# Turned maxima behind the products with v, an end in written order, and products beside the first steps of a fused block

## The chip, the cores and the metric

The kernel runs on one core of a Trainium2 chip. The metric is the device time of one execution in microseconds (us); lower is better. An execution is told by five engines that run side by side: PE (matrix products; PEld is its weight load), DVE (vector), ACT (scalar, activations), POOL (general), and SP, which only starts transfers here. Data lie in SBUF; PE writes only into the eight banks of PSUM, 128 x 512 numbers of 32 bits each, and DVE or ACT read them from there. All numbers are 32-bit floats.

## The reference

The input x has 8 batches of 1024 tokens of 256 features. One block with modulated layer norm is computed:

```python
mod = (silu(c) @ wmod).reshape(8, 6, 1, -1)
sa, ca, ga, sb, cb, gb = (mod[:, i] for i in range(6))
ga, gb = (sign(g) * max(abs(g), 0.25) for g in (ga, gb))
h = layernorm(x) * (1 + ca) + sa
x = x + ga * attention(h)        # 16 heads of 16, causal softmax, w_out, b_out
h = layernorm(x) * (1 + cb) + sb
x = x + gb * ffn(h)
# ffn: xp = x shifted by one token
# r = sigmoid((mu_r*x + (1-mu_r)*xp) @ Wr.T)
# k = relu((mu_k*x + (1-mu_k)*xp) @ Wk.T)**2 ; out = r * (k @ Wv.T)
```

## The kernel before

**Attention in units and steps.** A unit is four heads of one batch, so there are 32 units, 28 to 31 in the last batch (number 7). A unit's 1024 tokens are two chunks of 512 (c = 0 and 1). The scores are computed twice. `maxima` (pp) forms them with queries on the partitions and DVE takes each query's largest (`max`). `subtract` turns these maxima: a PE transpose into a bank (pmx), a copy with the sign turned to a row on ACT (mrow), and a small transfer that writes the row into row 16 of each head's strip of q, where k holds ones. `weights` (pw) then forms the scores with keys on the partitions, already less the maximum, and ACT takes the exponential from the bank into a tile w. `attend` multiplies w by v, extended by a column of ones that gives the sum (po), and copies the bank to a tile o on ACT, or to `more`, which POOL adds to o.

A unit takes nine steps, named a, b, c, d, e (pieces on the diagonal) and 0 to 3 (whole tiles). The maxima run LAG = 9 steps ahead of the weights, so a step as a rule holds the weights of one unit and the maxima of the next. Step numbers are counted from the first step of a batch's weights, 36 to a batch. The group of products with v that a step completes is written in the step after it (steps with c, e, 1 and 3; po_c, po_e and po). The last two units have other pieces (f, g, h, i) and groups.

**What stands in a step** (function `step`, line 1022): transfers that have come due (a transfer asked for by `later` goes out at the head of a later step, the rows of maxima first); the products of weights and maxima, in halves; after each half, exponentials and reductions; then the list `soon` (turned maxima among it, one step after the maxima are complete); then the fills of that step from the tables; then the products with v of the step before (`finish`, which calls `attend`). Maxima of chunk 0 are complete after the fifth step of the maxima, those of chunk 1 after the ninth. In every unit both turns fall into a step that also holds a group of products with v.

**Fills.** The rest of the block is cut into small pieces that tables place into numbered steps: START, PREP and PREP_FIRST (norm, turning, q, k, v of the next batch), POST, POST_LAST and END (projection py, second norm, mixing, receptance pr, key pk, value pkv). In a table, `n.q1` is a product q for the second chunk; x and y stand for the two chunks of the batch worked on. A step with no maxima and no fill gets five small transposes ("heat").

**Banks.** `bank` hands out four banks in rotation (tag t): pw, pmx, po and the fills use them. pp has four others, two to a tile (tag s). After the last maxima, `late` is set, and the fills take theirs from the tag s (`bank_apart`).

**Order.** Inside the steps `strict` is set, and then each engine's instructions are bound to the order in which they are written (class InOrder, line 113); PE is always bound so. The first instructions are bound by `start`. `tail` (line 860), which does the last chunk's projection, norm, mixing, key, value and output in two halves, was written with neither flag: PE follows the written order there, while the order on the other engines was left to the planner.

The first nine steps (LAG) have maxima only and the last nine have weights only. In such steps (`alone`) both halves are written at once.

Of the kernel before, what the change touches and what calls it, by code (L numbers as in the profile page):

```python
# [8 lines left out]
F32 = mybir.dt.float32  # L9
# [63 lines left out]
def adaln_block(  # L73
# [293 lines left out]
    def normalise(xt, S, tag, half):  # L367
        if half == 0:
            S["h"] = sb.tile([P, NT, D], F32, tag="h", bufs=2, name=f"h{tag}")
        h, mv, rs = S["h"], S["mv"], S["rs"]  # L370
        for t in (2 * half, 2 * half + 1):
            if strict[0]:
                act.activation(
                    h[:, t, :],
                    xt[:, t, :],
                    AF.Identity,
                    bias=S["away"][:, t : t + 1],
                    scale=rs[:, t : t + 1],
                )
            else:  # L380
                dve.tensor_scalar(
                    h[:, t, :],
                    xt[:, t, :],
                    mv[:, t, 0:1],
                    rs[:, t : t + 1],
                    ALU.subtract,
                    ALU.mult,
                )

    def transposed(h, to, b, d, shift, scale, name):  # L390

        pt = bank(name)
        for t in range(NT):
            pe.transpose(
                pt[:, t * P : (t + 1) * P], h[:, t, d * P : (d + 1) * P], ident
            )
        by, at = modT[:, scale, d, b : b + 1], modT[:, shift, d, b : b + 1]
        if d and shift == SHIFT_A:
            dve.tensor_scalar(to, pt, by, at, ALU.mult, ALU.add)
        else:  # L400
            act.activation(to, pt, AF.Identity, bias=at, scale=by)
# [246 lines left out]

    def attend(u, k):

# [10 lines left out]
        for m, (at, kt, lo, cols) in enumerate(parts):  # L661
            for j in range(HG):
                pe.matmul(
                    po[j * ST : (j + 1) * ST, lo:],
                    v_tile(b, kt)[:, (g * HG + j) * (HD + 1) :][:, :ST],
                    ws[at, j // 2][:, j % 2, cols],
                    start=m == 0,
                    stop=m == len(parts) - 1,
                )
        if ("o", c) not in V:  # L670
            V["o", c] = sb.tile([P, CW], F32, tag="o", bufs=3, name=f"o{u}_{c}")
# [95 lines left out]
    def post(b, c):  # L767
# [57 lines left out]
        def receptance(t0):  # L825
            pr = bank_apart(f"pr{b}_{c}_{t0}")
            rows(pr, S["mix"], wr_sb, (t0, t0 + 1))
            r = sb.tile([P, CW], F32, tag="r", bufs=2, name=f"r{b}_{c}_{t0}")
            act.activation(r, pr, AF.Tanh, scale=0.5)
            S["r", t0] = r  # L830
# [29 lines left out]
        def tail(other):  # L860

            def both(f):
                f(0)
                f(1)

            def columns(half):
                return slice(half * CW // 2, (half + 1) * CW // 2)

            both(lambda half: project(2 * half))
            other["multiplied0"]()
            st = sb.tile([P, NT, 6], F32, tag="st", bufs=2, name="st_last")
            mv = sb.tile([P, NT, 2], F32, tag="mv", bufs=2, name="mv_last")
            rs = sb.tile([P, NT], F32, tag="rs", bufs=2, name="rs_last")
            h = sb.tile([P, NT, D], F32, tag="h", bufs=2, name="h_last")

            def normal(half):
                ts = (2 * half, 2 * half + 1)
                for t in ts:  # L880
# [4 lines left out]
                pool.tensor_tensor(rs[:, of], rs[:, of], m_half[:, of], ALU.pow)  # L885
                if half:
                    pool.tensor_mul(away, mv[:, of, 0], rs[:, of])
                    pool.tensor_scalar_mul(away, away, -1.0)
                for n, t in enumerate(ts):
                    if half:  # L890
                        act.activation(
# [14 lines left out]
                    )  # L906

            away = sb.tile([P, 2], F32, tag="away", bufs=2, name="away_last")
            both(normal)
            h2T = sb.tile([P, DC, CW + 1], F32, tag="h2T", name="h2T_last")  # L910
            pool.tensor_copy(h2T[:, :, 0:1], A[b, 0]["edge"])

# [17 lines left out]

            turned(0)
            other["multiplied2"]()
            turned(1)
            step = sb.tile([P, DC, CW], F32, tag="step", name="step_last")
            S["mix"] = sb.tile([P, DC, CW], F32, tag="mix", bufs=2, name="mix_last")

            def mixed_half(half):
                of = columns(half)
                for d in range(DC):
                    dve.tensor_sub(  # L940
# [3 lines left out]
                    )  # L944
                for n in range(2):
                    for d in range(DC):
                        dve.scalar_tensor_tensor(
                            (S["mix"], step)[n][:, d, of],
                            step[:, d, of],
                            mus[:, n, d : d + 1],  # L950
                            h2T[:, d, of],
                            ALU.mult,
                            ALU.add,
                        )

            both(mixed_half)
            other["valued0"](), other["valued2"]()
            S["ka"] = sb.tile([P, DC, CW], F32, tag="mix", bufs=2, name="ka_last")

# [15 lines left out]

            both(lambda half: (receptance(2 * half), keys(half)))

            def values(half):
                t0 = 2 * half
                pv = bank(f"pkv_last{half}")  # L980
                rows(pv, S["ka"], G[b]["wv"], (t0, t0 + 1))
                r = S["r", t0]
                dve.scalar_tensor_tensor(r, r, 1.0, pv, ALU.add, ALU.mult)
                dve.tensor_add(flat(t0), flat(t0), r)
                (sync, act)[half].dma_start(
                    tokens(out, b, c)[:, t0 : t0 + 2, :], S["x"][:, t0 : t0 + 2, :]
                )

            both(values)

# [28 lines left out]

    soon = []  # L1020

    def step(T, T1, S, now, fill):
# [23 lines left out]
        for f in fill:  # L1046
            f()
        if not S and not fill:

            pt = bank_apart(f"heat{now}")  # L1050
            for n in range(5):
                pe.transpose(pt[:, :P], ident, ident)
        if T1 and T1[1] in groups_of(T1[0]):
            finish(T1, now)
        if S:
            u = S[0]
            for c, _, _ in STEPS[S[1]]:
                left[u, c] = left.get((u, c), PIECES[c]) - 1
                if left[u, c] == 0:
                    join(u, c)  # L1060
                    soon.append((now + 1, lambda c=c: subtract(u, c)))
        soon.sort(key=lambda z: z[0])

    def finish(T, now):
        u, k = T
        attend(u, k)
        c, _, ends = groups_of(u)[k]
# [44 lines left out]
    19 x.receptance0; 19 y.norm1; 20 y.turn; 20 x.receptance2; 20 x.key0; 21 y.mix; 22 x.key1;  # L1112
    22 y.mixed00; 24 y.mixed01; 24 y.mixed10; 24 x.value0; 25 y.mixed11; 26 x.value2;
    28 y.receptance0; 29 y.receptance2; 29 y.key0; 31 y.key1; 33 y.value0; 35 y.value2
    """

    POST_LAST = """
    -12 x.load; -6 x.bias; 4 x.project0; 6 x.project2; 7 x.stats0; 7 y.load; 8 x.stats1; 8 y.bias;
    9 x.norm0; 9 y.project0; 10 x.norm1; 10 x.turn; 11 x.mix; 11 y.project2; 12 x.mixed00;
    12 y.stats0; 13 x.mixed01; 13 x.mixed10; 13 x.receptance0; 14 x.mixed11; 15 x.receptance2;  # L1120
    15 y.stats1; 16 y.norm0; 17 x.key0; 17 y.norm1; 18 x.key1; 18 y.turn; 19 y.mix; 20 x.value0;
    20 y.mixed00; 21 y.mixed01; 21 y.mixed10; 22 x.value2; 22 y.mixed11; 22 y.receptance0;
    23 y.receptance2; 24 y.key0; 25 y.key1; 26 y.value0; 27 y.value2
    """
# [6 lines left out]
    START = """  # L1131
    0 n.turn; 3 m.q1; 4 m.k1; 6 n.q1; 7 n.k1; 8 m.v0; 10 m.v2; 11 n.v0; 13 n.v2
    """
# [3 lines left out]
    12 n.stats1; 13 n.norm0; 14 n.norm1; 15 n.turn; 16 n.q0; 17 n.k0; 19 m.v0; 20 m.v2; 20 m.q1;  # L1137
    22 m.k1; 22 n.q1; 24 n.k1; 29 n.v0; 31 n.v2
    """
    END = """  # L1140
    16 x.load; 18 x.bias; 26 y.load; 28 x.project0; 28 y.bias; 29 x.project2; 30 x.stats0;
    30 x.stats1; 31 x.norm0; 32 x.norm1; 32 x.turn; 33 x.mix; 34 x.mixed00; 34 x.mixed01;
    34 x.mixed10; 34 x.mixed11; 35 x.receptance0; 36 x.receptance2
    """
# [34 lines left out]
    for b in range(B):  # L1179
# [12 lines left out]
        )  # L1192
    place(END, at, x=ready[b][0], y=ready[b][1])

# [57 lines left out]
    finish(order_t[-1], len(slots))  # L1252
    for n, f in ((1, "key0"), (2, "key1")):
        soon.append((len(slots) + n, ready[B - 1][0][f]))
# [61 lines left out]
```

## Time and profile before

| | us |
|---|---|
| median of 3 executions | 1392.13 |
| lowest and highest | 1391.22 and 1395.94 |
| the profiled execution, whole | 1394.23 |
| its span, first to last instruction | 1392.5 |
| PE busy, share of the span | 1362.3, 98% |
| DVE, ACT, POOL busy | 1061.3, 876.1, 545.0 |
| one steady batch (from 383.46 to 547.16, and so on) | 163.7 |
| mean granted clock of PE | 0.996 |

The page gives busy time by engine, and the span in 40 slices with a digit for tenths of busy time. The timeline lists instructions in order of time: start, length, engine, line, operation, the tile written, `<-`, the tiles read, shapes, count, and in brackets the idle time of the engine ahead of it and what ended it. Nearly all instructions carry line 123, that of the helper InOrder, so tiles tell them apart. An end of a matrix product is modelled, and several run at once in parts of the array; the distance between starts tells more than the length. A stretch line gives its length and then busy time and count of PE, PEld, DVE, ACT and POOL, then the granted clock of PE (1.00 is full), the share of the transfer engines, and GB/s.

### The profile page before, as it was taken

The numbers are of one execution on the slowest core, as the hardware profiler recorded it, in microseconds if no ns is written. First come the engines' busy times: TensorE is split into PE (matmuls) and PEld (weight loads), VectorE is DVE, ScalarE is ACT, GpSimd is POOL, SyncE is SP. The second block draws the span as 40 slices with busy tenths as digits, with TensorE's granted clock in tenths as the row PEclk, the third lists the DMA queues.
The fourth block names the chain that finished last, engine by engine and source line by source line (L and its number), as shares of the span: only waits on it lengthen the run. The fifth ranks groups of instructions, "written<-read, shape, count | busy, mean of one in ns | idle before, by whom it ended". The sixth has DMA issues, their size and how long they took to land.

```text
span 1392.5 us, 29440 instructions
## 1 busy us (share of the span) xinstructions
PE 1362.3 (98%) x11093; PEld 751.1 (54%) x11093; DVE 1061.3 (76%) x2872; ACT 876.1 (63%) x1695; POOL 545.0 (39%) x841
## 2 busy tenths in 40 slices
PE   9999999999999999999999999999999999989997
PEld 5554455555555555555555555555555555555545
DVE  6787787788778777788777887778787877877624
ACT  3476676676666666665666666666666666556461
POOL 1142243345423454434434355234543344345432
PEclk9999999999999999999999999999999999999999
DMA  6513323232222323222242222323232222301101
GB/s 193 182 38 97 118 78 115 63 101 88 92 71 75 108 85 107 67 88 80 78 131 63 98 84 71 97 78 108 70 105 56 65 100 78 101 24 37 61 5 35
DMA packets 81582, 118.12 MB, mean 85 GB/s; under 512 B 10136, under 2 KB 39704, under 8 KB 81440
## 3 DMA queue, kind: packets, MB, share of 16 engines
q1 hardware_dynamic: 81104, 115.92, 25.9%
q8 instruction: 87, 1.43, 0.4%
q14 instruction: 55, 0.45, 0.1%
q10 hardware_dynamic: 336, 0.33, 0.1%
HBM read 70.63 MB, written 44.55 MB: 83 GB/s over the span
## 4 chain that ended last, share of the span: by engine, by line
PE 90%; DVE 4%; ACT 3%; POOL 1%; issue 1%; DMA 0%; ACTq 0%; DVEq 0%; POOLq 0%
PE pw L123 11%; PE po L123 8%; PE pq L123 8%; PE pp L123 7%; PE po_c L123 5%; PE po_e L123 5%; PE pr L123 4%; PE py L123 4%; PE pv L123 4%; PE pkv L123 4%; PE pk L123 4%; PE pw_a L123 3%; PE pw_e L123 3%; PE pw_c L123 2%; PE pw_b L123 2%; ACT w L123 2%
## 5 line engine op out<-in xcount | busy, mean ns | idle before, releaser
L123 DVE TENSOR_REDUCE max<-pp 128x2 f32<-128x1024 f32 x256 | 302.3, 1220 | 64.9 <-PE pp L123 64.4
L123 ACT ACTIVATE w<-pw 128x512 f32<-128x512 f32 x512 | 265.7, 602 | 82.8 <-PE pp L123 59.9
L123 PE MATMUL pw<-q,k 32*128 32x512 f32 x1024 | 267.4, 616 | 0.7 <-ACT w_i L123 0.6
L123 PE MATMUL pp<-k,q 32*128 32x512 f32 x1024 | 256.3, 619 | 0.4 <-DVE max L123 0.4
L123 PEld LDWEIGHTS pw<-q,k 32*128 32x128 f32 x1024 | 108.0, 183 | 101.3 <-issue 59.3
L123 DVE DVE_READ_ACCUMULATOR2_ANT max<- 128x1 f32 x1024 | 144.7, 141 | 0.0
L123 DVE CUSTOM_DVE_ANT_0 pp_c<-pp_c,mask 128x256 f32<-128x256 f32 x240 | 102.3, 436 | 42.6 <-PE pp_c L123 36.5
L123 DVE CUSTOM_DVE_ANT_0 pp_b<-pp_b,mask 128x128 f32<-128x128 f32 x240 | 102.3, 437 | 38.3 <-PE pp_b L123 32.1
L123 DVE CUSTOM_DVE_ANT_0 pp_e<-pp_e,mask 128x512 f32<-128x512 f32 x128 | 88.0, 708 | 54.7 <-PE pp_e L123 52.6
L123 DVE CUSTOM_DVE_ANT_0 pp_d<-pp_d,mask 128x128 f32<-128x128 f32 x240 | 102.4, 437 | 30.2 <-PE pp_d L123 24.1
L123 PE MATMUL po<-w,v 128*32 128x512 f32 x1024 | 123.1, 598 | 1.2
L123 PE MATMUL pq<-hT,wqk_sb 128*128 128x512 f32 x240 | 115.3, 613 | 0.0
L123 DVE CUSTOM_DVE_ANT_0 pp_a<-pp_a,mask 128x512 f32<-128x512 f32 x128 | 87.8, 707 | 11.6 <-PE pp_a L123 9.5
L123 POOL TENSOR_TENSOR xb<-xb,r 128x512 f32<-128x512 f32 x30 | 38.9, 1298 | 141.3 <-DVE r L123 116.2
L123 ACT ACTIVATE w_a<-pw_a 128x512 f32<-128x512 f32 x128 | 66.5, 603 | 41.5 <-PE pp_a L123 38.0
L123 POOL TENSOR_TENSOR o<-o,more 128x512 f32<-128x512 f32 x62 | 78.6, 1267 | 35.7 <-ACT more L123 35.6
L123 POOL TENSOR_TENSOR rsb<-rsb,m_half 128x2 f32<-128x2 f32 x30 | 21.4, 714 | 172.3 <-DVE rsb L123 171.0
L123 PEld LDWEIGHTS pp<-k,q 32*128 32x128 f32 x1024 | 83.8, 184 | 6.5 <-DVE max L123 4.5
L123 ACT ACTIVATE w_d<-pw_d 128x512 f32<-128x512 f32 x120 | 62.4, 601 | 22.8 <-PE pp_e L123 20.6
L123 ACT ACTIVATE w_e<-pw_e 128x512 f32<-128x512 f32 x128 | 66.1, 603 | 15.7 <-PE pp_c L123 13.5
L123 ACT ACTIVATE w_b<-pw_b 128x512 f32<-128x512 f32 x120 | 62.0, 602 | 18.5 <-PE pp L123 18.0
L123 PEld LDWEIGHTS pq<-hT,wqk_sb 128*128 128x128 f32 x240 | 42.7, 191 | 52.0 <-issue 35.4
(212 smaller groups left out, 3002.0 us busy)
## 6 DMA issues: line engine op xcount, KB each, us to landing
pad<-qk SPq DMA_DIRECT2D x60, 256.0 KB
q<-pad SPq DMA_DIRECT2D x30, 512.0 KB
k<-pad SPq DMA_DIRECT2D x30, 512.0 KB
od<-o SPq DMA_DIRECT2D x60, 256.0 KB
xa<-in_x SPq DMA_DIRECT2D x16, 512.0 KB
xb<-in_x SPq DMA_DIRECT2D x16, 512.0 KB
oT<-od SPq DMA_DIRECT2D x60, 128.0 KB
ov<-over SPq DMA_DIRECT2D x30, 256.0 KB
```

Source lines behind the costliest of these rows:

```text
L123: made = f(*args, **kwargs)
```

## The change

There are three parts.

The turning of maxima goes into a list of its own, `turns`, and is called from inside `attend`, behind the products with v and ahead of the copy of o; in a step that has no such products, behind the fills. So pmx follows po on PE, mrow stands ahead of the copy of o (or more) on ACT, and the transfer follows at the head of the next step as before.

The tables place pieces anew: in START a product stands beside each of the maxima steps 3 to 8; POST exchanges value0 and mixed pieces; in POST_LAST and END the projections, statistics, norms and mixing of the last two batches come one or two steps earlier, y's keys and values come two to six steps later, and the receptance of the second half of x goes behind the last products with v.

The tail is bound to written order on all engines and written anew: half 0 is normalised by ACT and half 1 by DVE (before, the other way round); the mixing is in another order; the values of the last half are cut into two tiles of tokens, each with its own transfer; the receptances take tiles of the tag w. In the last nine steps and the tail, normalising and one of two copies of the turned half move from ACT to DVE.

```diff
@@ normalise, transposed
-            if strict[0]:
+            if strict[0] and not late[0]:
                 act.activation(
...
-        if d and shift == SHIFT_A:
+        if d and (shift == SHIFT_A or late[0]):
             dve.tensor_scalar(to, pt, by, at, ALU.mult, ALU.add)
@@ attend
-    def attend(u, k):
+    def attend(u, k, then):
...
+        then()
         if ("o", c) not in V:
             V["o", c] = sb.tile([P, CW], F32, tag="o", bufs=3, name=f"o{u}_{c}")
             act.copy(V["o", c], po)
@@ step
+        def turned_maxima():
+            while turns and turns[0][0] <= now:
+                turns.pop(0)[1]()
+
         if T1 and T1[1] in groups_of(T1[0]):
-            finish(T1, now)
+            finish(T1, now, turned_maxima)
+        turned_maxima()
...
-                    soon.append((now + 1, lambda c=c: subtract(u, c)))
+                    turns.append((now + 1, lambda c=c: subtract(u, c)))
@@ tail: order of the parts
-            both(lambda half: project(2 * half))
-            other["multiplied0"]()
-            both(normal)
-            turned(0)
-            other["multiplied2"]()
-            turned(1)
-            both(mixed_half)
-            other["valued0"](), other["valued2"]()
-            both(lambda half: (receptance(2 * half), keys(half)))
-            both(values)
+            start[0] = True
+            project(0)
+            normal(0)
+            project(2)
+            normal(1)
+            other["multiplied0"]()
+            turned(0)
+            other["multiplied2"]()
+            turned(1)
+            late[0] = False
+            mixed_half(0)
+            mixed_half(1)
+            receptance(0)
+            keys(0)
+            other["valued0"](), other["valued2"]()
+            receptance(2)
+            keys(1)
+            values(0)
+            values(1)
@@ tail: normal
-                if half:
+                if half == 0:
                     pool.tensor_mul(away, mv[:, of, 0], rs[:, of])
                     pool.tensor_scalar_mul(away, away, -1.0)
@@ tail: values
+                for ts in ((t0,), (t0 + 1,)) if half else ((t0, t0 + 1),):
...
+                    (act if ts[0] == NT - 1 else sync).dma_start(
@@ tables
 POST       24 mixed01; 24 mixed10; 24 x.value0; 25 mixed11; 26 x.value2
         -> 24 x.value0; 24 mixed01; 25 mixed10; 26 mixed11; 26 x.value2
 POST_LAST  x.project0 4 -> 2; x.project2 6 -> 5; x.stats 7, 8 -> 6, 7; x.norm 9, 10 -> 8, 9;
            x.receptance0 13 -> 14; y.key0 24 -> 26; y.key1 25 -> 30; y.value0 26 -> 31;
            y.value2 27 -> 33
 START      n.q1 6 -> 5; n.k1 7 -> 6; m.v0 8 -> 7; m.v2 10 -> 8
 PREP_FIRST n.k1 24 -> 25
 END        x.stats0 30 -> 29; x.norm0 31 -> 30; x.norm1, x.turn 32 -> 31; x.mix 33 -> 32;
            x.mixed00 34 -> 32; x.mixed01, 10, 11 34 -> 33; heat at 34;
            x.receptance2 36 -> behind finish
@@ behind the last step
-    for n, f in ((1, "key0"), (2, "key1")):
+    for n, f in ((1, "receptance2"), (2, "key0"), (2, "key1")):
         soon.append((len(slots) + n, ready[B - 1][0][f]))
```

## The prediction

> **What bounds the kernel now.** I read the page's engine totals and slices first.
>
> ```profile
> PE 1362.3 (98%) x11093; PEld 751.1 (54%) x11093; DVE 1061.3 (76%) x2872; ACT 876.1 (63%) x1695; POOL 545.0 (39%) x841
> PE   9999999999999999999999999999999999989997
> DVE  6787787788778777788777887778787877877624
> ```
>
> TensorE is the bound from the second slice to the thirtieth; only the last ten slices thin out. A steady batch lasts 163.7 us and shows 1.2 us of idle PE, so a gain has to come out of time that counts as busy. The timeline of PE and ScalarE in one step shows where that is:
>
> ```profile
> 883.95 0.49 PE L123 MATMUL pp_d<-k,q 32*128 32x384 f32 x2
> 884.39 0.28 PE L123 MATMUL pmx<-ident,max 128*16 128x128 f32 x1
> 884.89 1.07 PE L123 MATMUL po_e<-w_e,v 128*32 128x512 f32 x8 [0.23 <-ACT w L123]
> ...
> 887.18 0.70 PE L123 MATMUL pw<-q,k 32*128 32x512 f32 x2
> ...
> 883.66 2.25 ACT L123 ACTIVATE w<-pw 128x512 f32<-128x512 f32 x4 [0.51 <-PE pp_d L123]
> 885.80 0.25 ACT L123 ACTIVATE mrow<-pmx 16x128 f32<-16x128 f32 x1
> 887.31 0.59 ACT L123 COPY o<-po_e 128x512 f32<-128x512 f32 x1 [1.27 <-PE po_e L123]
> ```
>
> pmx is the turning of maxima, po_e the products with v. pw, pmx and po draw on the same four PSUM banks. pmx takes the first bank that the exponentials free, po must wait for the second: 0.50 us from the start of pmx to po_e. The list of PE's waits repeats it:
>
> ```profile
> PE po_e L123 <- ACT w L123: 5.8, 25, 0.2
> ```
>
> Then the ends: PE's waits and the granted clock (the column after the five engines, in the stretches).
>
> ```profile
> 40.77 2.26 PE L123 MATMUL pp<-k,q 32*128 32x512 f32 x8 [0.42 <-DVE max L123]
> 42.96 3.44 PE L123 MATMUL pq<-hT,wqk_sb 128*128 128x512 f32 x4
> ...
> 1230.69 0.33 PE L123 MATMUL ptb<-ident,hb 128*128 128x128 f32 x1 [1.51 <-ACT hb L123]
> ...
> 1246.65 1.56 PE L123 MATMUL pr<-wr_sb,mix 128*128 128x256 f32 x6 [1.73 <-DVE mix L123]
> ...
> 1374.93 1.39 PE L123 MATMUL pt_last<-ident,h_last 128*128 128x128 f32 x4 [2.83 <-ACT h_last L123]
> ```
>
> ```profile
> 1372.00:1374.00 2.00, 0.10 (x1) 0.00 (x0) 2.00 (x5) 0.00 (x0) 1.73 (x4) 1.00 0.00 0
> 1374.00:1376.00 2.00, 1.05 (x4) 0.76 (x5) 1.15 (x3) 1.09 (x2) 1.40 (x2) 0.64 0.00 0
> 1376.00:1378.00 2.00, 2.00 (x7) 1.64 (x6) 1.01 (x3) 1.02 (x2) 0.28 (x1) 0.51 0.38 131
> ```
>
> Each of the three waits of 0.42, 1.51 and 2.83 us has a stretch of half clock behind it (about 43.3 to 46.6, 1231.6 to 1235, 1374.6 to 1378); the wait of 1.68 us at 1363 has none.
>
> **The turning of maxima (A).** 64 transposes (0.28 us), 64 row copies on ScalarE (0.25) and 64 small transfers keep their number and go behind po. By starts in PE's timeline, 25 turns ahead of po_e cost 0.50 or 0.51 us; 25 ahead of the other po cost 0.31 (18) or 0.37 (7). The rest, where no bank is waited for, cost 0.20 or 0.21, or 0.11 ahead of a full-height product (pmx 1322.79, py 1322.91). Behind po the turn has the second bank, free by then; I charge 0.21, as it still stands between two kinds of tiling. Gain 25 x 0.295 + 25 x 0.117 = 10.3 us. Upper end at 0.11 a turn: 15.3. Lower end 0, as the wait can return in full at the next step, whose second half needs the banks of po and pmx; it cannot cost more there, since the same copies free them. Timed on the step above: po from 884.39, its end at 886.6, pmx to 886.9, row copy 886.92 to 887.17, the copy of o behind it to 887.66; the second half of the next step comes about 0.98 after its first, at 887.8. DVE, done with pp_d at 887.76, frees the other buffer at the same moment. So 0.3 is all there is; a further shift would meet DVE.
>
> The row's transfer is first on SP's queue in the next step, now about 1.1 us later; behind it wait od<-o, pad<-qk and the loads, each read a step or more later. On ScalarE the fills' work (hb, 1.07 us) now stands ahead of the row, the copy of o behind it. The first reader of a row of chunk 1 is pw_c, 6.0 us after pmx started in a steady unit. New: row copy done 2.4 us after that old start, issue 0.6, travel 2.2 (as oT<-o on the final chain), 0.24 to PE: 5.5. In time by 0.4. In three units pw_c comes 5.08, 4.00 and 4.11 us after pmx: late by about 0.3, 1.4, 1.3; DVE covers part, I charge 2.0. A: -8.3.
>
> **The first steps (B).** v0, v2, q1 and k1 are the same work one to two steps earlier, so step 5 has a product and step 10 none. Gone: the wait 0.42 and the half-clock cost 3.44 - 1.99 = 1.45. Step 10 keeps 2 us of pairs beside 2.36 of reduction: new wait 0.4. B: -1.5, between -2.4 (were that wait covered too) and 0 (half clock at step 10 instead).
>
> **The last batch (C).** PE's waits between 1189 and 1264 sum to 0.82 + 0.61 + 0.32 + 1.51 + 0.15 + 0.20 + 1.73 = 5.3, half clock costs 1.7. With project0 two steps earlier (py 1.92) it lies in the wait for DVE at step 3; step 4 then has no product, and DVE's 4.2 us on pp_c end last. Carried step by step (DVE's reductions 2.36 to 4.2 a step, stats 1.4, py 0.69), the gain is lost again by step 9; the normalised half then stands a step before its turn, which removes 1.51 and the half clock; receptance0 one step later removes most of 1.73, DVE's mixed steps keeping 1 us. Steps 1 to 18: -3.8. In steps 24 to 27 (6.1, 4.2, 6.6 and 3.9 us) the products of y leave, four of 1.92, one returning in step 26; DVE (3.4, 2.4) and exponentials (2.07 plus a copy 0.59) hold the steps at 4.2, 2.5, 7.0, 2.4 to 2.9: -4.3 by step 29. Steps 30, 31 and 33 take three back, 5.8 us against some 2 us of waits and with the turn out of step 32; receptance2 (1.9) leaves for the wait of 1.68 behind the finish. Net -2.2. Bounds: -11 if all waits go, 0 if DVE keeps them all. C: -6.0.
>
> **The tail (D).** Up to 1368.2 the chain stays: po, o, psum, pinv, o, oT<-o, py, xb, stats; receptance2 is as long as the key it replaces there. Half 0 now goes through POOL (0.20 + 0.30) and ScalarE (1.09): h at 1370.8, 1.0 later. Half 1 no longer stands behind r<-r,pkv, POOL's xb (1.46) and the slow rs: statistics follow the second xb at 1368.8, pow to 1371.0, h on DVE to 1371.7 where ScalarE ended at 1375.4. multiplied2 (1.7) is written ahead of its turn, so that starts at 1373.1 (before 1374.93). Then ACT to 1375.05, six DVE steps of 0.43 to 1377.65, four PE products of 1.71 from 1374.2 without gap to 1381.05, values to 1384.45, last add 1385.9, issue and landing 3.0 (3.4 before, for twice the bytes): end 1388.9 against 1392.5. out<-xb of the other chunk moves from 1376.3 to about 1382.1, 512 KB at 350 GB/s, over by 1384.7; the last issue comes after. D: -3.6, between -5 (turn not delayed by multiplied2) and 0 (half clock on the products, DVE late).
>
> **Sum.** -8.3 - 1.5 - 6.0 - 3.6 = -19.4. The profiled execution took 1394.2 (span 1392.5), so 1374.8; it was 2.1 above the median of the runs shown: 1372.7, rounded to 1373. POST's exchange of value0 and mixed steps I cost at nothing: the same DVE work inside the same steps, covered by 20% of free DVE; 1 us a batch if not.
>
> [...]
>
> **The rivals.** (1) The bank wait only moves: the second half of the next step waits for the copy of o behind the row copy. For it: my timing leaves 0.1 us. Against: ScalarE is idle 1.27 us there. A becomes +2.0: 1383. (2) The ends give nothing, since DVE and the half clock take back what the tables move. For it: DVE is 81% busy from 1180 to 1220 while PE waits; against: the 2.83 and 1.51 waits have visible causes that the order removes. Only A and B: 1382. (3) Slower: the row of chunk 1 lands late. It has 0.4 us to spare in 24 units; one 512 KB load ahead of it on the rings (1.5 us at 350 GB/s) makes pw_c wait 1.1 us in each, +26 us: 1399. It decides against the change from a landing about 1.4 us later than worked out. Against it: the row is first on SP's queue in its step.
>
> **How the numbers follow.** Forecast 0.62, (1) 0.17, (2) 0.13, (3) 0.05, and 0.03 for (1) and (2) together, 1392. About 0.3% (4.2 us) is what a measurement of this kernel can tell. Faster: 0.62 + 0.17 + 0.13 = 0.92; same 0.03; slower 0.05. At the bottom the range takes A's upper end (1368) and half of what C's bound adds (1365); at the top it reaches past (1) and (2) to (1) with most of C gone (1387).
>
> **What would show it.** Right: po_e starts 0.44 after the last pp_d and pmx behind it at 0.1 to 0.2; a batch lasts 162.1 instead of 163.7; no half clock at 43; ptb without wait at step 10; pt_last without 2.83. Wrong: pw waits for ACT o or mrow in the second half, pw_c for the transfer of the row; the batch still at 163.7; half clock in the tail.

## The result and the profile after

The changed kernel takes 1373.97 us (median of 4 runs, 1372.52 to 1375.23); the kernel before, run beside it, 1391.68. The ratio is 0.9866, with a 95% interval of 0.9843 to 0.9888. The profiled execution of the changed kernel took 1373.32 us with a span of 1370.7, against 1394.23 and 1392.5 before: 21.8 us of span. The forecast was 1373. The sum is right, in part by luck: several of its terms are not.

The page's engine totals and slices of the changed kernel:

```profile
PE 1357.8 (99%) x11103; PEld 747.6 (55%) x11103; DVE 1065.7 (78%) x2879; ACT 873.4 (64%) x1690; POOL 547.1 (40%) x841
...
PE   9999999999999999999999999999999999999998
```

PE has lost 4.5 us of busy time and 17.3 of idle time. The last slices are full now. The list of PE's waits of the changed kernel (what PE waited for, total us, times, longest) shows what went and what came:

```profile
PE pw_c L123 <- DMA q<-mrow: 1.8, 1, 1.8
PE pt_last L123 <- ACT h_last L123: 0.9, 2, 0.8
```

The 25 waits of po_e, the wait of pr, that of py and those of ptb are gone from the list, and pt_last has 0.9 us left of 2.8. One wait is new: pw_c, in the first unit, for a row of maxima. The timeline of the changed kernel where a unit's maxima are turned:

```profile
878.21 0.64 PE L123 MATMUL po_e<-w_c,v 128*32 128x256 f32 x8
878.64 0.42 PE L123 MATMUL po_e<-w_d,v 128*32 128x128 f32 x8
878.99 0.28 PE L123 MATMUL pmx<-ident,max 128*16 128x128 f32 x1
879.20 0.70 PE L123 MATMUL pw<-q,k 32*128 32x512 f32 x2
...
879.31 0.27 ACT L123 ACTIVATE mrow<-pmx 16x128 f32<-16x128 f32 x1 [1.28 <-PE pmx L123]
879.48 0.56 ACT L123 COPY o<-po_e 128x512 f32<-128x512 f32 x1
```

The turn costs 0.21 us here, and 0.20 or 0.21 in all 64 turns, and the products of the next step start without a wait. Now the new wait, in the timeline of the first unit (the last two lines are the transfers that SP starts: first the strips that are cleared, then the row):

```profile
58.70 0.37 PE L123 MATMUL pw_c<-q,k 32*128 32x256 f32 x1
60.91 0.65 PE L123 MATMUL pw_c<-q,k 32*128 32x256 f32 x2 [1.84 <-DMA q<-mrow]
...
52.98 2.39 SPq L123 DMA_DIRECT2D pad<-k  x2
56.41 0.56 SPq L123 DMA_DIRECT2D q<-mrow  x1
```

The row is asked for at 56.41 and read at 60.91, 4.5 us later.

**Where the time went.** Where two kernels have the same instructions, their traces agree to 0.01 us a step (the changed kernel and that of experiment 12 stay 1.57 to 1.59 us apart at the 28 turns from 758 to 1305 us), so the two can be laid beside each other at the start of each step. Up to 158 us, in the first batch, the changed kernel is 0.2 us behind, and at 172 us 1.1 behind. From there to the second step of the last batch (1177 us) it gains 13.2: 2.2 a batch, which is more than the 1.3 to 1.4 that the eight turns of a batch give (four of 0.27 to 0.30, four of 0.03 to 0.12). The tables of the last batch give 5.6 up to the last psum (the PE product that turns the last sums; the tail is counted from it), the tail 4.1. Where a stretch of half clock lies in one of the two, it is still in these numbers.

These stretches have to be taken out before the parts are summed. Each lasts 3.4 us or twice that, and one of 6.8 us costs 3.28 (measured below), so I charge 1.64 for 3.4 us. The profile before has three of them ahead of the end of PE's work (43, 1231, 1375 us), the profile after one (61 us). Without them the spans are 1387.6 and 1369.1, 18.5 us apart. This charge is an upper value: where another profile has the same code without the stretch, 3.4 us cost 1.2 us at 43 (against experiment 3), 1.2 at 61 (against experiments 4, 10 and 12, with the row's wait taken out), 1.5 at 1231 (experiment 1 against 11, which have the same wait there) and 1.2 at 1375 (against the end of experiment 1). With these the two are 19.1 us apart. The three stretches of the profile before are more than most executions of that kernel have: of the 29 that were timed beside the experiments, 21 have a granted clock of 0.998 or 0.999 and take 1390.9 to 1392.3 us, and 8 have 0.994 to 0.997, like this profile with its 0.996, and take 1393.0 to 1396.9.

### The profile page after: what moved, and what is told of

It is laid out like the page before. It is cut to its first block, busy times and chain, and to the rows that moved or that the text cites. A ratio compares the mean times of both kernels' runs of the same rounds, so it can differ in the third digit from the quotient of the medians.

```text
span 1370.7 us, 29487 instructions
## 1 busy us (share of the span) xinstructions
PE 1357.8 (99%) x11103; PEld 747.6 (55%) x11103; DVE 1065.7 (78%) x2879; ACT 873.4 (64%) x1690; POOL 547.1 (40%) x841
## 4 chain that ended last, share of the span: by engine, by line
PE 94%; DVE 3%; DMA 1%; issue 1%; POOL 0%; ACT 0%; SPq 0%; DVEq 0%; ACTq 0%; POOLq 0%
PE pw L123 12%; PE po L123 9%; PE pq L123 8%; PE pp L123 7%; PE po_c L123 5%; PE po_e L123 5%; PE pr L123 4%; PE py L123 4%; PE pv L123 4%; PE pk L123 4%; PE pkv L123 4%; PE pw_a L123 3%; PE pw_e L123 3%; PE pw_c L123 2%; PE pw_d L123 2%; PE pw_b L123 2%
## 5 line engine op out<-in xcount | busy, mean ns | idle before, releaser
L123 PE MATMUL pw<-q,k 32*128 32x512 f32 x1024 | 262.0, 616 | 0.0
L123 PEld LDWEIGHTS pw<-q,k 32*128 32x128 f32 x1024 | 104.8, 183 | 97.2 <-issue 39.5
L123 POOL TENSOR_TENSOR xb<-xb,r 128x512 f32<-128x512 f32 x30 | 41.9, 1397 | 137.4 <-DVE r L123 111.4
L123 PEld LDWEIGHTS pp<-k,q 32*128 32x128 f32 x1024 | 78.6, 183 | 3.7 <-DVE max L123 3.6
L123 PEld LDWEIGHTS po<-w,v 128*32 128x32 f32 x1024 | 26.7, 109 | 84.5 <-issue 41.6
L123 ACT ACTIVATE w_c<-pw_c 128x512 f32<-128x512 f32 x120 | 62.4, 603 | 14.8 <-PE pp_b L123 9.9
```

Source lines behind the costliest of these rows:

```text
L123: made = f(*args, **kwargs)
```

## The experiments

"Without half clock" below means the span less 1.64 us for each stretch of 3.4 us, which can be 0.4 too much for each. Each profile is one execution; a median is over the runs of that kernel. The changed kernel was not timed again beside the later ones; the kernel before was, at 1391.7 to 1392.1 each time.

**1. The turning alone, in the kernel before.**

```diff
+        then()                                   # attend, behind po
...
-            finish(T1, now)
+            finish(T1, now, turned_maxima)
+        turned_maxima()
...
-                    soon.append((now + 1, lambda c=c: subtract(u, c)))
+                    turns.append((now + 1, lambda c=c: subtract(u, c)))
```

> The kernel before with the turning of maxima behind the products with v, and nothing else of the change. Theory (the bank wait is gone for good: pmx to the next product 0.21 us in all 64 turns, no new wait): about 9.0 us faster than the kernel before, a steady batch of 162.3 us instead of 163.7. Rival (the wait only moves to the second half of the next step, behind the copy of o): 0 to 2 us slower, the batch stays at 163.7. In the first unit the row now goes out 1 us later, but with the old table a product of 1.9 us still stands in step 10, so a wait of pw_c of at most 0.3 us is expected there.

Measured: 1386.15 us, ratio 0.9953 (0.9939 to 0.9967), some 6 us faster; a steady batch takes 162.3 us, and without half clock the spans differ by 6.4. From the second unit to the last batch each turn of chunk 0 gives 0.27 to 0.30 us, each of chunk 1 0.03 to 0.12, 8.9 in all once the 3.3 us of a half-clock stretch at 113 us are taken out. That is the theory's 9. But about 2.5 us are given back elsewhere (8.9 less 6.4), or 1.6 with the smaller costs of single stretches (a difference of 7.3). Two waits give 1.5 of that. In the first unit pw_c waits 1.17 us for the row, although the product stands ahead of it; the expectation had allowed for 0.3. In the last batch, at 1321 us, pw waits 0.93 us for a row, where it waited 0.62 for ScalarE before.

**2. All but the turning.** In the changed kernel:

```diff
-                    turns.append((now + 1, lambda c=c: subtract(u, c)))
+                    soon.append((now + 1, lambda c=c: subtract(u, c)))
```

> The changed kernel with the turning back in the list of the step, ahead of the products with v. Theory (the parts add up): 8 to 10 us slower than the changed kernel, so 11 to 13 us faster than the kernel before; in the first unit the row goes out about 1.0 us earlier, and pw_c's wait of 1.84 us shrinks to about 0.8. Rival (the new tables already took the wait on the second bank away, so that the turning adds nothing beside them): within 2 us of the changed kernel.

Measured: 1377.79 us, 3.8 slower than the changed kernel; 5.2 without half clock. Between the second unit and the last batch the turning is worth 8.1 us; at the start it costs 1.8, as the row is in time again here (PE has no wait for it), and in the last two units about 0.8 us. What makes up that last part I did not follow. So the rival, that the tables had already taken the bank wait away, is out, and the theory's 8 to 10 are too many: what the turns give in the middle is right, and the late row is the difference.

**3. The exchange in POST alone.** In the kernel before:

```diff
-    22 y.mixed00; 24 y.mixed01; 24 y.mixed10; 24 x.value0; 25 y.mixed11; 26 x.value2;
+    22 y.mixed00; 24 x.value0; 24 y.mixed01; 25 y.mixed10; 26 y.mixed11; 26 x.value2;
```

> The kernel before with only the table POST exchanged (value0 ahead of mixed01, mixed10 and mixed11 one step later). Theory from the two traces (step 24 of a steady batch takes 3.78 us instead of 4.72): 0.78 us a batch in six batches, so 4.7 us faster than the kernel before, and a batch of 162.9 us. Rival, the price of the prediction (the same work of DVE inside the same steps, covered by its free 20%): 0, the batch at 163.7.

Measured: 1388.63 us, ratio 0.9975 (0.9963 to 0.9988), 1.7 to 5.1 us faster. In the trace one step falls by 0.95 us in each of the six batches and the next unit gives 0.05 back, 5.4 in all; nothing else in between moves by more than 0.02. The timed gain is smaller: the nine executions have a granted clock of 0.992 to 0.997, where those of the kernel before mostly have 0.999, so they held more half clock. The fills of step 24 stand behind its products, so DVE does them while PE is in step 25; the step that falls is PE's step 25, although the expectations call it step 24. DVE at that point of a steady batch, the kernel before:

```profile
809.34 0.74 DVE L123 SCALAR_TENSOR_TENSOR mix<-step,mus,h2T 128x512 f32<-128x512 f32 x1
810.00 0.75 DVE L123 SCALAR_TENSOR_TENSOR step<-step,mus,h2T 128x512 f32<-128x512 f32 x1
810.66 0.68 DVE L123 SCALAR_TENSOR_TENSOR r<-r,pkv 128x512 f32<-128x512 f32 x1
811.26 1.22 DVE L123 TENSOR_REDUCE max<-pp 128x2 f32<-128x1024 f32 x1
```

and the changed kernel:

```profile
803.27 0.69 DVE L123 SCALAR_TENSOR_TENSOR r<-r,pkv 128x512 f32<-128x512 f32 x1 [0.39 <-PE pkv L123]
803.88 0.75 DVE L123 SCALAR_TENSOR_TENSOR mix<-step,mus,h2T 128x512 f32<-128x512 f32 x1
804.54 2.35 DVE L123 TENSOR_REDUCE max<-pp 128x2 f32<-128x1024 f32 x2
```

In the kernel before, three fills and two reductions on DVE (the second, 1.23 us, at 812.68) take 4.62 us together, and PE's step, from its first weights at 809.66 to those of the next step at 814.38, takes 4.72. In the changed kernel there are two fills and the same two reductions, 3.79 us, and the step takes 3.78 (803.17 to 806.95). In the kernel before PE is held in the middle of the step: the rotation of four banks gives a score product of its second half the bank of pkv, which r<-r,pkv frees. That ends at 811.34, and the product goes at 811.47 instead of about 810.6; PE shows no idle time there, as another product runs. (An exponential ends at 811.42, and the profile puts the wait down to it.) In the changed kernel PE's products follow each other without a gap, and DVE is idle for 0.39 us. So before the step is as long as DVE makes it, and after it is as long as PE's own work.

**4 and 5. Which half of that exchange.** In the changed kernel, first the old order with the new load, then the new order with the old load:

```diff
-    22 y.mixed00; 24 x.value0; 24 y.mixed01; 25 y.mixed10; 26 y.mixed11; 26 x.value2;
+    22 y.mixed00; 24 y.mixed01; 24 x.value0; 25 y.mixed10; 26 y.mixed11; 26 x.value2;
...
+    22 y.mixed00; 24 x.value0; 24 y.mixed01; 24 y.mixed10; 25 y.mixed11; 26 x.value2;
```

> The changed kernel with value0 behind mixed01 again in step 24, while mixed10 and mixed11 stay at 25 and 26: of the exchange in POST only the moved load is left. Theory (what counts is the DVE work that left step 24): step 24 keeps its 3.8 us, within 0.2 of the changed kernel's in each of six batches. Rival (what counts is that value0's work on DVE stands ahead of the mixing, as r<-r,pkv frees a bank): step 24 goes back to 4.7 us, a batch to 162.4 us, 5 us slower in all.

> The changed kernel with mixed10 back in step 24 and mixed11 back in 25, value0 still ahead of them: of the exchange in POST only the order is left. Theory (the moved load is what counts): step 24 goes back to 4.5 to 4.7 us, a batch to 162.3, about 5 us slower in all than the changed kernel. Rival (the order counts): step 24 keeps 3.8 us and the batch 161.5.

Measured, against the changed kernel: the old order costs 0.16 us a batch, the old load 0.67. Together that is the 0.8 which the exchange gives beside the new turning. So the moved load is the larger part, and the order alone gives little. Why the old load costs 0.67 even in the new order is less clear than the theory has it. In experiment 5 r comes first, the bank is free in time and PE's step 25 keeps 3.79 us; it is step 26 that takes 4.67 instead of 3.85. And the instruction that was put back takes 1.78 us instead of 0.75, while POOL does an addition that in the kernel before starts only when this instruction is over (811.42 against 810.75):

```profile
810.19 1.78 DVE L123 SCALAR_TENSOR_TENSOR step<-step,mus,h2T 128x512 f32<-128x512 f32 x1
809.69 1.73 POOL L123 TENSOR_TENSOR xb<-xb,r 128x512 f32<-128x512 f32 x1 [6.48 <-DVE r L123]
```

How much of the 0.67 is the load and how much this longer instruction was not tried. (The one time of each, 1372.01 and 1380.09, says less: in the second, pw_c waited 3.8 us for the row and 6.8 us of half clock followed, in code that is the same in both.)

**6. The product back at step 10.**

```diff
-    0 n.turn; 3 m.q1; 4 m.k1; 5 n.q1; 6 n.k1; 7 m.v0; 8 m.v2; 11 n.v0; 13 n.v2
+    0 n.turn; 3 m.q1; 4 m.k1; 5 n.q1; 6 n.k1; 7 m.v0; 10 m.v2; 11 n.v0; 13 n.v2
```

> The changed kernel with the first table's m.v2 back at step 10 (5 n.q1, 6 n.k1 and 7 m.v0 stay), so that a product of 1.9 us stands ahead of the products that wait for the late row. Theory (the first steps lost 4.4 us because the row takes 4.4 us to land and nothing is left to cover it, and the half clock came with that wait): the wait of 1.84 us is under 0.3 us, no stretch of half clock behind 61 us, 2 to 4 us faster than the changed kernel. Rival (the row isn't what holds this step, DVE's 4.2 us of reductions are): the wait comes back under another name, within 1 us of the changed kernel.

Measured: 1372.57 us, 1.4 under the changed kernel's median, and 0.7 of span; half missed. The wait of 1.84 is gone. But the product had been covering something at step 8, too: there PE now waits 0.47 us for DVE. The first weights start 2.2 us earlier, and 1.5 of that is lost again by 79 us, where the product now stands. And the half clock came all the same, at 57 us, though that wait of 0.47 had ended 5.3 us ahead.

**7. The clearing transfers out of the row's way.**

```diff
-    for n, m, half in ((1, 0, 1), (4, 1, 0), (6, 1, 1), (8, 0, 0)):
+    for n, m, half in ((1, 0, 1), (4, 1, 0), (6, 1, 1), (11, 0, 0)):
```

> The changed kernel with the four transfers of 256 KB that clear the last quarter of the padded strips (fill at step 8) moved to step 11, behind the step in which the first unit's second row goes out. Theory (the row takes 4.4 us to land because these transfers stand ahead of it on the rings): the row lands about 2 us after its issue, pw_c's wait of 1.84 us is gone, 1.5 to 2 us faster than the changed kernel from the first weights to the third unit. Rival (the row is slow for another reason, such as the loads q<-pad and k<-pad issued behind it): it still lands about 4 us after its issue and the wait stays at 1.5 us or more. A stretch of half clock in the first 70 us can still come or not come with either, at about 1.3 us.

Measured: 1371.46 us (1368.91 to 1374.01), and 1.7 us less from the first weights to 79 us without half clock: the wait is gone, so it was these transfers. The first weights start 1.5 us later here, behind a stretch of half clock at 11.8 us that no other profile has. This profile then loses 3.28 us again, at 1193 us, where PE's instructions are the same as in the changed kernel:

```profile
1190.00:1192.00 2.00, 2.00 (x13) 0.91 (x12) 1.90 (x10) 1.50 (x4) 0.52 (x2) 1.00 0.14 9
1192.00:1194.00 2.00, 2.00 (x12) 0.80 (x8) 1.86 (x10) 1.08 (x2) 0.00 (x0) 0.70 0.39 148
1194.00:1196.00 2.00, 2.00 (x6) 1.24 (x5) 1.84 (x8) 0.00 (x0) 0.00 (x0) 0.50 0.10 39
1196.00:1198.00 2.00, 2.00 (x6) 1.29 (x4) 0.64 (x3) 0.00 (x0) 0.00 (x0) 0.50 0.00 0
1198.00:1200.00 2.00, 2.00 (x13) 0.52 (x16) 0.69 (x1) 0.00 (x0) 0.00 (x0) 0.60 0.01 4
```

These are stretches of 2 us (length; busy time and count of PE, PEld, DVE, ACT, POOL; granted clock; share of the transfer engines; GB/s). PE is busy throughout, ahead of the drop as behind it, and the clock is at half for 6.8 us.

**8. The same with the product of PREP_FIRST back at step 24.**

```diff
-    22 m.k1; 22 n.q1; 25 n.k1; 29 n.v0; 31 n.v2
+    22 m.k1; 22 n.q1; 24 n.k1; 29 n.v0; 31 n.v2
```

> The same, and the first preparation table's n.k1 back from step 25 to step 24, so that step 24 of the first batch holds a product again. Theory (without it PE waits for DVE in that step): another 0.9 us between the steps before and behind, so 2.4 to 2.9 us faster than the changed kernel, about 1371. Rival (the product only takes as long as the wait that it fills): 0 from this edit.

Measured: 1368.72 us (1368.10 to 1369.32), ratio 0.9823 (0.9802 to 0.9844), the fastest of all. The edit of PREP_FIRST is worth 0.83 us, that of the transfers 1.7; the rest of the 4.1 us of span is the half-clock stretch, which this profile does not have. The first unit in its timeline:

```profile
58.81 0.37 PE L123 MATMUL pw_c<-q,k 32*128 32x256 f32 x1
58.92 0.69 PE L123 MATMUL pw_c<-q,k 32*128 32x256 f32 x3
...
56.52 0.57 SPq L123 DMA_DIRECT2D q<-mrow  x1
57.14 1.21 SPq L123 DMA_DIRECT2D pad<-q  x2
```

The row is read 2.4 us after it is asked for, or less, where it took 4.5 with the clearing transfers ahead of it.

**9. The row behind the copy of o.** `then()` moved to the end of `attend`.

```diff
-        then()
         if ("o", c) not in V:
...
+        then()
```

> The changed kernel with the turning of maxima behind the copy of o (or more) instead of ahead of it: PE's order stays, on ACT mrow comes 0.5 us later and the copy of o 0.2 us earlier. Theory (the bank wait is gone because pmx follows po, whatever ACT does next; the row has 1 to 2 us to spare in a steady unit, as only the fifth product of pw_c reads it): a steady batch stays at 161.5 us within 0.2; in the first unit pw_c waits up to 0.5 us longer. Rival (the spare time is only the 0.4 us that the prediction worked out): pw_c waits about 0.1 to 0.2 us in each unit and the batch is 0.5 to 1 us longer.

Measured: one time, 1371.56 us; the batch is 0.04 us shorter and no unit but the first waits for a row (1.5 us there). The order on ScalarE does not matter here: neither the bank of po nor the row was short. The prediction's rival 1 has nothing to stand on.

**10 and 11. The last batch undone.** In the changed kernel, the table END, the place of receptance2 and the late norm and copy as before; then POST_LAST as before, too.

```diff
-    for n, f in ((1, "receptance2"), (2, "key0"), (2, "key1")):
+    for n, f in ((1, "key0"), (2, "key1")):
...
-            if strict[0] and not late[0]:
+            if strict[0]:
...
-    8 x.norm0; 9 x.norm1; 9 y.project0; 10 x.turn; 11 x.mix; 11 y.project2; 12 x.mixed00;
+    9 x.norm0; 9 y.project0; 10 x.norm1; 10 x.turn; 11 x.mix; 11 y.project2; 12 x.mixed00;
```

> The changed kernel with the last table END, the place of receptance2 and the late norm and copy (ACT instead of DVE) as before; POST_LAST and the tail stay new. Theory (steps 24 to 37 of the last batch gave 2.2 us through this part and the keys and values of y together): 2 to 4 us slower than the changed kernel at the last psum. Rival (the keys and values of y, which stay moved here, gave it and END only trades): within 1 us.

> The same with POST_LAST as before too, so that all tables of the last batch are undone and the tail stays new. Theory (the two traces: 3.4 us in steps 1 to 18, 2.2 us in steps 24 to 37): 5.6 us slower than the changed kernel at the last psum, with the waits of ptb (1.5 us) and pr (1.7 us) back and half clock behind ptb's. Rival (waits of DVE take back what the tables move): within 2 us.

Measured: END is worth 2.8 us at the last psum (the one time, 1373.49 us, does not show it: this profile has no half clock ahead of the end). With POST_LAST undone, too, 1378.14 us, 4.2 slower than the changed kernel; 7.7 at the last psum in the trace, of which 3.3 are a half-clock stretch of 6.8 us at 1324. So the tables are worth 4.4 us, 1.6 of them in steps 1 to 18; the rivals, 1 and 2 us, are out, and the first theory's 5.6 are too many. Two of the waits that this kernel has again:

```profile
1218.95 0.33 PE L123 MATMUL ptb<-ident,hb 128*128 128x128 f32 x1 [1.44 <-ACT hb L123]
...
1233.40 1.56 PE L123 MATMUL pr<-wr_sb,mix 128*128 128x256 f32 x6 [1.70 <-DVE mix L123]
```

No half clock follows the 1.44 us here, and the expectation had counted 1.7 us for one.

**12. The tail undone.** The changed kernel with the whole function `tail` as before.

```diff
-            start[0] = True
-            project(0)
-            normal(0)
-            project(2)
-            normal(1)
...
+            both(lambda half: project(2 * half))
+            other["multiplied0"]()
...
+            both(normal)
```

> The changed kernel with the tail as before: no written order on the other engines, half 1 normalised by ACT behind the slow rs, values in two halves. Theory (its order is what took 4.1 us off the end): the span from the last psum to the end grows from 30.8 to 34 to 35 us, pt_last waits 2.8 us again, 3 to 4 us slower than the changed kernel; with a stretch of half clock 1.3 us more. Rival (the end was shortened by the receptance moved ahead of it, not by its order): within 1 us.

Measured: 1376.18 us, 2.2 slower than the changed kernel. In the trace 4.5 us are lost behind the last psum, 2.8 of them without the stretch of half clock that follows:

```profile
1355.63 0.33 PE L123 MATMUL pt_last<-ident,h_last 128*128 128x128 f32 x1 [2.81 <-ACT h_last L123]
...
1356.51 1.80 PE L123 MATMUL pr<-wr_sb,mix_last 128*128 128x256 f32 x4
```

```profile
1357.00:1358.00 1.00, 1.00 (x4) 0.81 (x3) 0.66 (x2) 0.73 (x2) 0.00 (x0) 0.50 0.05 18
1358.00:1359.00 1.00, 1.00 (x4) 0.72 (x4) 1.00 (x4) 0.00 (x0) 0.00 (x0) 0.50 1.02 350
```

The new tail, and not the receptance moved ahead of it, is what shortens the end. Which of its parts does it, the written order, the exchange of the halves or the last values in two pieces, was not tried one by one.

## Why the prediction came out right

Sizes in us, minus for a gain; "runs" are without half clock:

| step | prediction | profile, after less before | runs |
|---|---|---|---|
| A, turning, in the turns | -10.3 | -8.1 to -8.9 | -8.1, -8.9 |
| A, late rows | +2.0 | +1.8 in the first unit, about 0.8 in the last ones | +2.5 (1.6 with the smaller costs), +2.9 |
| B, first steps | -1.5 | with the first unit's late row 0.2 to the bad | -1.4 with the row in time |
| PREP_FIRST's product | none | +0.87 | +0.83 |
| POST's exchange | 0 | -4.7 to -5 | -5.4 alone, -5.0 beside the turning |
| C, last batch | -6.0 | -5.6 | -4.4 |
| D, tail | -3.6 | -4.1 | -2.8 |
| half clock | inside B, C, D | -3.3 by the flat charge, inside C and D | differs by execution |

**A.** The mechanism was right. Behind po the second bank is free, the turn costs the 0.21 that was charged, and neither the next step's second half nor pw_c of a steady unit waits; experiment 9 shows that there was more room than the 0.1 and 0.4 us that were worked out, as only the fifth product of pw_c reads the row. The gain of a turn of chunk 1 was put at 0.117 and is 0.03 to 0.12. The charge of 2.0 for late rows was of the right size and at the wrong place: the units it was made for lost nothing, and the first unit, which was not looked at, lost 1.8.

**B.** This is the step that failed. The sum has "step 10 has none" and a "new wait 0.4" for DVE. It does not ask what the product at step 10 was hiding. It hid the first unit's row, which stands behind 1 MB of clearing transfers in the same queue. That is rival 3, a row that lands late, whose price was worked out for 24 steady units and whose place is the one unit with another load ahead of it. In the kernel before, pw_c of that unit comes 6.1 us after its turn, and the product of 1.9 us that B takes away is part of that time. With the row in time the steps give 1.4 up to 158 us (experiment 2, one stretch of half clock in each profile) and 1.4 up to the second unit (experiment 8, with 1.2 taken off for the stretch at 43); with the late row (the change) they give nothing. It is luck that this is close to the forecast's 1.5. The forecast was 0.42 and 1.45 less 0.4, nearly all half clock, and without half clock it was nothing. The gain has another source: the steps ahead of the first weights take in one product more at no cost. The first weights start at 51.91 us in experiment 3, with one product v ahead of them, and at 51.77 in experiment 2, with two; neither has half clock up to there. The step that gives the product away becomes shorter.

**PREP_FIRST.** Moving n.k1 by a step was named in the change and left out of the sum. It leaves step 24 of the first batch without a product. The step becomes 2.0 us shorter (1.88 against 3.89 in experiment 8) and the next one, which has the product of 1.9 now, 2.8 longer (6.62 against 3.78): its score products are held up beside four reductions on DVE, 4.81 us in a row, while PE shows no idle time. That loses 0.83 us.

**POST.** "Covered by 20% of free DVE" is the other step that failed, by 4.7 to 5.0 us to the good. The 20% are a mean over the batch; for the step behind step 24 DVE had 4.62 us of work in 4.72 us, and the step was as long as DVE made it, while PE counted as busy. It is also not the same work inside the same steps: two instructions go one step later. The hedge in that sentence, 1 us a batch, is close to the 0.8 that came.

**C and D.** The order of gains and their places were right: 1.44 to 1.51 us ahead of ptb, 1.7 ahead of pr, 2.81 ahead of pt_last go, and the tail's chain ends with PE unbroken from 1353.2 to 1364.8. Where they were too large, the half clock that they count is about as much. C counted 1.7 us for the stretch behind ptb's wait; 6.0 less 1.7 is 4.3, and the runs have 4.4: 1.6 in steps 1 to 18, against 3.8 less 1.7, and 2.8 from END, against 2.2 for all that stands behind step 23. D's 3.6 was taken against a tail that had such a stretch in it. The 350 GB/s that D and rival 3 reckon with is in the trace of the kernel before: the 512 KB of out<-xb asked for at 1376.3 move from 1377.2 to 1378.8 us, in most slices of 0.1 us at 328 to 379 GB/s.

**The half clock** was read as a consequence of each wait, and it follows such a wait only at times. The same code with the same wait of 0.42 us, in the kernel of experiment 3:

```profile
41.24 2.26 PE L123 MATMUL pp<-k,q 32*128 32x512 f32 x8 [0.42 <-DVE max L123]
43.43 1.13 PE L123 MATMUL pq<-hT,wqk_sb 128*128 128x512 f32 x2
```

```profile
44.00:45.00 1.00, 1.00 (x4) 0.34 (x2) 0.77 (x1) 0.00 (x0) 0.00 (x0) 1.00 0.53 205
```

In the profile before, half clock follows that wait, and four of these products take 3.44 us, where two take 1.13 here. The gain of 1.45 us in B was thus drawn by lot, and so were those in C and D in part. The sum also takes half clock off twice: the profile lies 2.1 us above the median, which by the granted clocks above is its half clock, and B, C and D count the same stretches as gains. The rivals' working stays as it was: 1 is out by experiments 1 and 9, 2 by 10 to 12, and 3 is real in one unit of 32.

The total came out because terms cancel. Against the forecast's 19.4, the two profiles without half clock have 18.5 to 19.1: POST gave 5 us that were not in the sum, while A, B, PREP_FIRST, C and D together fell short by some 5 to 6, most of it half clock that the forecast had counted (1.45, 1.7 and, at the end, some 1.2). Two slips decide nothing: the row's time adds up to 5.44 us, so 0.56 to spare and not 0.4; and B's terms allow -1.9 at the lower end, not -2.4. The batch, put at 162.1 us, is at 161.5, and the difference is POST's.

## What to carry to other kernels

Before a piece of work is moved out of a step, ask what it was covering there, transfers that are on their way included, and look at the first and last rounds one by one: the price of a late row was worked out for 24 equal units and paid in the odd one. A share of free time over a batch says nothing about one step (20% here, and 4.62 us of work in a step of 4.72); where two engines hand buffers to and fro, count the busy time of the second engine within that step against the step's length, also while the first engine shows as busy, and look at the step behind it too. And read a gain that rests on one profiled execution's half clock as one draw, not as a part of the change.

## What the runs showed of the hardware

In these profiles half clock on PE (a granted clock of 0.50) came in pieces of 3.4 us (three in the profile before, one in that after), or two of them in a row (6.8 us, in experiments 1, 5, 7 and 11). Profiles whose code is the same at one place had it there or not, and executions of one kernel differed in its amount (granted clock 0.996 to 0.999 in the four of the changed kernel). Behind the row's wait in the first unit (1.5 to 3.8 us, seven profiles with the new table and the new turning) it came four times; behind ptb's 1.4 to 1.5 us in three of four; behind pt_last's 2.8 in three of four; behind the 0.33 to 0.42 at step 6 in one of three; behind 0.76 ahead of a ptb of the last steps (at 1316 to 1335 us) in two of five. In experiments 2 and 6 it came at 57 us, 2.9 and 5.3 us behind waits of 0.09 and 0.47. Twice it came with PE busy and no idle time above 0.1 us in the 20 us ahead: at 113 us in experiment 1 and at 1193 us in experiment 7, where 6.8 us of it cost 3.28 us against the same instructions at full clock. What brings such a stretch on is not shown by these runs.

A small transfer was the first that its step asked for and still waited: in the first unit the row of 8 KB took 4.5 us to be read with four transfers of 256 KB asked for in the 6 us ahead of it, and 2.4 or less with them behind it. Steps that shared code took the same time to 0.01 us each (the changed kernel and that of experiment 12 keep their distance to 0.02 us over 546), so two executions laid beside each other by the starts of their steps show an edit of 0.16 us a batch which their times, 1372.52 to 1375.23 us for one kernel, can't.
